# The seam between 50 recurrent steps and the score stores: counting on VectorE in the last step, both centrings first on ScalarE, and a later first split

## The chip, the cores and the metric

The kernel runs on one core of one Trainium2 chip. A core has TensorE (PE) for matrix products and transposes, VectorE (DVE), ScalarE (ACT) and GpSimd (POOL) for elementwise work, SyncE (SP), which here only issues transfers, and 16 DMA engines that carry them out. Matrix products land in PSUM; the other tiles on the core are in SBUF. The metric is the time of one execution on the device in microseconds (us).

## What is computed

A batch of 1024 sequences of 50 item numbers is turned into scores against 100001 items. Cut to what matters:

```python
emb = emb_table.at[0].set(0.0)                  # 100001 x 128
prefix = jnp.cumsum(emb[seq], axis=1)           # 1024 x 50 x 128
uF = prefix / jnp.minimum(t_idx, lengths)       # running mean of the items so far
y = (uF - mean) * rsqrt(var + 1e-5) * gamma + beta   # over the batch, for each step and feature
def step(v, x):                                 # 50 steps
    v = v + (x - v) / 2
    spike = (v - 1 >= 0)
    return v - spike, spike
scores = spikes.mean(axis=0) @ emb.T            # 1024 x 100001, 409.6 MB
```

Each step needs the one before it, since v is carried. The scores need the spike counts of all 50 steps.

## The kernel before

**Layout.** In the recurrent part the 128 features are the partitions and the 1024 sequences are the columns, so the mean and the variance over the batch are reductions along a row. v lives in PSUM (in turn in `v0` and `v1`), the counts in a bfloat16 tile `count`, and `negv` is the negative of v after its spikes are taken off. The order on each engine is as written in the program; nothing reorders it, and a semaphore wait is added wherever an instruction needs another engine's result, a buffer that is still read, or a PSUM bank that another engine is at.

**A step t.** Eight gathers of GpSimd (`gather`, L196) bring the rows of step t, two steps ahead, into one of two buffers `e`. PE transposes them onto the running sum `pre` (L309), which is two tiles of 512 columns, one for each half of the batch. VectorE makes `uF` from each half (L318) and its statistics (L319), then aggregates them to `mv` (L329). ScalarE takes a square root (L333) and centres `uF` (L340). VectorE makes the scale `a` by three tiny instructions, ScalarE applies it (`x`, L363), VectorE counts the spikes of the previous v (`spiked`, L289) and makes the new one (`step`, L366), and ScalarE makes `d`, v minus the threshold in bfloat16 (`over`, L282). `rest` (L286) on VectorE makes `negv` from d and v in the next step.

**The last step.** It is written apart, so that the first scores can start early. At its top GpSimd makes `s` from d (L303) and adds it to `count` (L304), which takes over the count of step 48's spikes. Between the two halves VectorE does `rest` and then `near` (L323), a piece of 128 columns that the first product needs. After `mv`, the first 128 sequences are finished by VectorE alone (`centred`, `vA`, `countA`); the other 896 go in two pieces, which ScalarE centres (L402) and scales (L363) one after the other, and which VectorE steps and counts into `countB` and `countC` (L366, L289). Sixteen transposes `warm` (L398) keep PE busy meanwhile.

**The scores.** The table is split into 98 parts of 1024 items. `prepare` transposes a part's rows on PE into PSUM (L124), ScalarE rounds them to a `hi` part (L146), and VectorE makes the remainder `lo` (L147); a product of 128 sequences by 512 items is two matmuls, with hi and with lo (`product`, L154). The first two parts are prepared inside steps 42 and 44. Blocks n of 128 sequences are worked through for groups of columns `WIDTHS`: the first groups have two parts, so a block is 128 x 2048. VectorE and ScalarE in turn scale 1024 columns from PSUM to an output tile `o` (L483, L485), and SyncE's queue issues its store (`store`, L163). Block 0 of the first group stands apart: four pieces of 512 columns, three scaled by ScalarE (L419) and the last by VectorE (L417), each stored at once. Block 1 stores 1024 columns at a time and later blocks the whole tile. There are four output tiles in the first groups, used in turn; a tile is refilled when its store has landed. `ready` prepares the next part when a hi and lo pair is free. In the first group one pair is free, so one part, the third, is prepared after block 2's store (L494), and the fourth when block 7 has set a pair free.

Of the kernel before, what the change touches and what calls it, by code (L numbers as in the profile page):

```python
# [12 lines left out]
F32 = mybir.dt.float32  # L13
# [5 lines left out]
ALU = mybir.AluOpType  # L19

P = 128
BN_EPS = 1e-5
V_TH = 1.0
HALF = 1024
KQ = HALF // P
BANK = 512
# [10 lines left out]
def rec_kernel(  # L37
# [124 lines left out]
    def store(n, c0, o):  # L162
        nc.sync.dma_start(out=outs[n, :, c0 : c0 + o.shape[1]], in_=o)  # L163


    with ExitStack() as ph:
# [118 lines left out]
        def rest(d, v):  # L285
            nc.vector.scalar_tensor_tensor(negv, d, 0.0, v, ALU.is_ge, ALU.subtract)  # L286
# [11 lines left out]
        for t in range(T):  # L298
            last = t == T - 1
            e = es.pop(t)  # L300
            if last:
                s = once.tile([P, B], F32, tag="zT", name="s")
                nc.gpsimd.tensor_single_scalar(s, d, 0.0, ALU.is_ge)  # L303
                nc.gpsimd.tensor_tensor(count, count, s, ALU.add)  # L304
            uF = up.tile([P, B], F32, tag="uF", name=f"uF_{t}")
            bs = sp.tile([P, B // BANK, 6], F32, tag="bs", name=f"bs_{t}")
            for h, cs in enumerate(halves):
                for k in range(0, BANK, P):
                    nc.tensor.matmul(  # L309
                        pre[h][:, k : k + P],  # L310
                        lhsT=e[:, h * BANK + k : h * BANK + k + P],
                        rhs=ident,
                        start=False,
                        stop=last,
                        is_transpose=True,
                        skip_group_check=True,
                    )
                nc.vector.scalar_tensor_tensor(uF[:, cs], rlen[:, cs], 1.0 / (t + 1), pre[h], ALU.max, ALU.mult)  # L318
                nc.vector.bn_stats(bs[:, h, :], uF[:, cs])  # L319
                if last and h == 0:  # L320
                    rest(d, v)
                    near = once.tile([P, P], F32, tag="r0", name="near")
                    nc.vector.tensor_scalar(near, negv[:, :P], -0.5, hgb[:, 1:2], ALU.mult, ALU.add)  # L323
            if t + 2 < T:
                gather(t + 2)
            if not last:
                correct(t + 1, l)
            mv = sp.tile([P, 2], F32, tag="mv", name=f"mv_{t}")
            nc.vector.bn_aggr(mv, bs.rearrange("p h s -> p (h s)"))  # L329


            r = sp.tile([P, 1], F32, tag="r", name=f"r_{t}")
            nc.scalar.activation(r, mv[:, 1:2], AF.Sqrt, bias=eps)  # L333
            if last:
                centred = once.tile([P, P], F32, tag="r0hi", name="centred")
                nc.vector.tensor_scalar(centred, uF[:, :P], mv[:, 0:1], hgb[:, 2:3], ALU.subtract, ALU.mult)
                w = sp.tile([P, 1], F32, tag="w", name="w")
                nc.vector.tensor_scalar_add(w, mv[:, 1:2], BN_EPS)
            else:
                nc.scalar.activation(uF, uF, AF.Identity, bias=mv[:, 0:1], scale=-1.0)  # L340


            if t and not last:
                rest(d, v)

            nc.vector.reciprocal(r, r)
            q = sp.tile([P, 1], F32, tag="q", name=f"q_{t}")
            a = sp.tile([P, 1], F32, tag="a", name=f"a_{t}")
            if last:
                nc.vector.tensor_scalar(q, w, r, r, ALU.mult, ALU.mult)  # L350
                nc.vector.scalar_tensor_tensor(q, q, 3.0, r, ALU.subtract, ALU.mult)
                vA = once.tile([P, P], F32, tag="r0n", name="vA")
                nc.vector.scalar_tensor_tensor(vA, centred, q, near, ALU.mult, ALU.add)
                spiked(countA, slice(0, P), vA)
                nc.vector.tensor_mul(a, q, hgb[:, 0:1])
            else:
                nc.vector.scalar_tensor_tensor(q, mv[:, 1:2], BN_EPS, r, ALU.add, ALU.mult)
                nc.vector.tensor_scalar(q, q, r, 3.0, ALU.mult, ALU.subtract)
                nc.vector.tensor_scalar(a, q, r, hgb[:, 0:1], ALU.mult, ALU.mult)


            def x(vt, cs):
                nc.scalar.activation(vt, uF[:, cs], AF.Identity, bias=hgb[:, 1:2], scale=a)  # L363

            def step(vt, cs):
                nc.vector.scalar_tensor_tensor(vt, negv[:, cs], -0.5, vt, ALU.mult, ALU.add)  # L366

            if not last:
                vt = vp.tile([P, B], F32, tag=f"v{t % 2}", name=f"v_{t}")
                x(vt, whole)  # L370
                if t:
                    spiked(count, whole, v)
                step(vt, whole)
                v = vt
                d = over(t, v)
                if t + 2 < T:
                    l = only(t + 2)

                if t in (T - 8, T - 6):
                    q = (t - T + 8) // 2  # L380
                    pair(q)
                    prepare(q, vp.tile([P, HALF], F32, tag="v1", name=f"pt_{q}"))
                    if q == TWICE - 1:
                        for k in range(TWICE):
                            rows[GROUP + k] = first[:, k, :]
                        nc.sync.dma_start(
                            out=first[:, :TWICE, :],
                            in_=table[GROUP * HALF : (GROUP + TWICE) * HALF, :].rearrange(
                                "(q p k) d -> p q (k d)", p=P, k=KQ
                            ),  # L390
                        )
# [8 lines left out]
        groups = [(slice(P, P + BANK), pre[1], countB), (slice(P + BANK, B), vC, countC)]  # L400
        for cs, vt, _ in groups:
            nc.scalar.activation(uF[:, cs], uF[:, cs], AF.Identity, bias=mv[:, 0:1], scale=-1.0)  # L402
            x(vt, cs)
        for cs, vt, c in groups:
            step(vt, cs)
            spiked(c, cs, vt)


        po0 = accp.tile([P, HALF], F32, tag="po0", name="po_0_0")
        po1 = vp.tile([P, HALF], F32, tag="v0", name="po_0_1")  # L410
        for q, (pool, tag, po) in enumerate(((gp, "e", po0), (up, "uF", po1))):
            o = pool.tile([P, HALF], F32, tag=tag, name=f"o_0_{q}")
            for h, cs in enumerate(halves):
                product(po[:, cs], q, 0, h * BANK, BANK)
            for h, cs in enumerate(halves):
                if q and h:
                    nc.vector.tensor_scalar_mul(o[:, cs], po[:, cs], 1.0 / T)  # L417
                else:
                    nc.scalar.mul(o[:, cs], po[:, cs], 1.0 / T)  # L419
                store(0, q * HALF + h * BANK, o[:, cs])  # L420

# [15 lines left out]
    for c, W in enumerate(WIDTHS):  # L439
# [30 lines left out]
        for n in range(NB):  # L470
            if c == 0 and n == 0:
                continue
            pool, tag, most = turns[blocks % len(turns)]
            blocks += 1
            o = pool.tile([P, most * HALF], F32, tag=tag, name=f"o_{c}_{n}")
            for q in range(q0, q1):
                h0 = (q - q0) * HALF
                hw = size(q)
                po = psum.tile([P, HALF], F32, tag="ps", name=f"po_{n}_{q}")
                for k0 in range(0, hw, BANK):  # L480
                    product(po[:, k0 : k0 + BANK], q, n, k0, min(BANK, hw - k0))
                if turn % 2 == 0:
                    nc.vector.tensor_scalar_mul(o[:, h0 : h0 + hw], po[:, :hw], 1.0 / T)  # L483
                else:
                    nc.scalar.mul(o[:, h0 : h0 + hw], po[:, :hw], 1.0 / T)  # L485
                turn += 1
                if c == 0 and n == 1:
                    store(n, q * HALF, o[:, h0 : h0 + hw])
                if n == NB - 1:
                    free.append(split.pop(q))  # L490
                    ready()
            if c or n > 1:
                store(n, q0 * HALF, o[:, : min(N, q1 * HALF) - q0 * HALF])
            if 2 <= n < NB - 1:  # L494
                ready()

            if n in (1, 4) and c >= MIDDLE and to_fetch < parts:
                g, k = divmod(to_fetch - TWICE, GROUP)
                if k or to_split >= (g - 1) * GROUP + TWICE:
                    if k == 0:  # L500
                        r = group(g)
                    fetch(r, to_fetch, GROUP // 2)
                    to_fetch += GROUP // 2
# [21 lines left out]
```

## Time and profile before

| | us |
|---|---|
| median of three timed runs (lowest, highest) | 1579.63 (1579.41, 1580.53) |
| the profiled execution | 1638.67 |
| its span, first to last instruction | 1636.5 |
| busy in the span: PE, VectorE, ScalarE, GpSimd | 1090.1, 942.9, 668.0, 388.3 |
| time of the chain that ended last spent on the score stores | 44% |
| mean rate of the transfers | 298 GB/s |

The profiled execution is 3.7% longer than the timed runs, so a time from the profile is used for differences and not for the whole. In the timelines below, times are microseconds from the start of the span; a row gives start, duration, engine, line, operation and operands, and in square brackets how long the engine had idled before and what released it. "remote" is a releaser that the profile couldn't name. The seam between the two stages is at about 577 us of this profile.

### The profile page before, as it was taken

What the parts mean: (1) busy time and instruction counts of PE and PEld (TensorE: products, weight loads), DVE (VectorE), ACT (ScalarE), POOL (GpSimd) and SP (SyncE); (2) the same over time, 40 slices, a digit from 0 to 9 for tenths busy, and PEclk for the clock granted to TensorE, in tenths of its full rate; (3) what the DMA queues carried; (4) which work ended last, traced back from release to release, by engine and by line L of the source; (5) the groups of instructions that cost most, each with busy time, mean ns of one, the idle gap of its engine ahead of it and who ended that gap; (6) DMA issues with size and microseconds to landing.
All of it is one profiled execution on the core that took longest, in us unless ns stands there. A gap on an engine that the chain in (4) does not pass through costs nothing.

```text
span 1636.5 us, 12239 instructions
## 1 busy us (share of the span) xinstructions
PE 1090.1 (67%) x4450; PEld 809.3 (49%) x4450; DVE 942.9 (58%) x1125; ACT 668.0 (41%) x697; POOL 388.3 (24%) x408
## 2 busy tenths in 40 slices
PE   4332334333343489898988788888778887888884
PEld 2111112111122267666866667666666666666663
DVE  5675667665575866565755555555545555555552
ACT  2332333333333355455544444444444444444442
POOL 7666676666766600000000000000000000000000
PEclk9999999999997599999999998999999999899998
DMA  9511111111112189999999999999999999999998
GB/s 347 213 47 45 45 50 48 45 45 47 52 45 59 51 358 416 402 421 414 409 423 435 427 429 423 419 429 425 413 429 412 429 421 420 426 411 417 412 427 344
DMA packets 51897, 488.12 MB, mean 298 GB/s; under 512 B 10075, under 2 KB 11004, under 8 KB 30588
## 3 DMA queue, kind: packets, MB, share of 16 engines
q1 hardware_dynamic: 30464, 429.81, 62.5%
q0 software_dynamic: 12800, 26.24, 6.0%
q10 hardware_dynamic: 8572, 31.28, 4.8%
q8 instruction: 35, 0.57, 0.1%
q14 instruction: 26, 0.21, 0.0%
HBM read 77.69 MB, written 409.60 MB: 298 GB/s over the span
## 4 chain that ended last, share of the span: by engine, by line
DMA 47%; PE 12%; DVE 11%; POOL 10%; another core or an unknown queue 7%; issue 6%; ACT 6%; ACTq 0%; SPq 0%; DVEq 0%; POOLq 0%
DMA scores<-o 44%; PE po L154 11%; POOL e L196 10%; ACT o L485 4%; DVE bs L319 2%; DVE uF L318 2%; DMA rows<-in_L_rec_emb_table 2%; DVE v L366 2%; DVE negv L286 1%; DMA e<-in_L_rec_emb_table,idx 1%; DVE o L483 1%; DVE count L289 1%; ACT v L363 1%; PE pt L124 1%
## 5 line engine op out<-in xcount | busy, mean ns | idle before, releaser
L483 DVE TENSOR_SCALAR o<-po 128x1024 f32<-128x1024 f32 x391 | 464.6, 1220 | 348.1 <-DMA scores<-o 313.8
L485 ACT ACTIVATE o<-po 128x1024 f32<-128x1024 f32 (+1 forms) x391 | 389.3, 1018 | 541.7 <-DMA scores<-o 326.3
L196 POOL DMA_INDIRECT e<-in_L_rec_emb_table,idx x400 | 382.7, 957 | 178.9 <-issue 115.9
L154 PE MATMUL po<-pairs,countB 128*128 128x512 f32 x1136 | 305.7, 415 | 64.2 <-ACT o L485 47.3
L154 PEld LDWEIGHTS po<-pairs,countB 128*128 128x128 f32 x1136 | 219.0, 198 | 126.9 <-ACT o L485 61.7
L154 PE MATMUL po<-pairs,countC 128*128 128x512 f32 x852 | 235.6, 423 | 47.3 <-ACT o L485 47.2
L270 PE MATMUL pre<-zT,ls 128*128 128x512 f32 x100 | 78.9, 791 | 257.1 <-DVE uF L318 211.3
L154 PEld LDWEIGHTS po<-pairs,countC 128*128 128x128 f32 x852 | 166.2, 201 | 92.8 <-ACT o L485 58.4
L309 PE MATMUL pre<-ident,e 128*128 128x128 f32 x400 | 129.3, 438 | 90.6 <-DMA e<-in_L_rec_emb_table,idx 70.7
L270 PEld LDWEIGHTS pre<-zT,ls 128*128 128x128 f32 x100 | 29.7, 298 | 294.8 <-DVE uF L318 238.2
L318 DVE SCALAR_TENSOR_TENSOR uF<-rlen,pre 128x512 f32<-128x512 f32 x100 | 68.0, 680 | 167.4 <-remote 126.8
L309 PEld LDWEIGHTS pre<-ident,e 128*128 128x128 f32 x400 | 79.9, 207 | 141.5 <-DMA e<-in_L_rec_emb_table,idx 107.7
L147 DVE TENSOR_TENSOR pairs<-pt,pairs 128x1024 fp32r<-128x1024 f32 x71 | 86.2, 1221 | 93.8 <-ACT pairs L146 93.7
L333 ACT ACTIVATE r<-mv,eps 128x1 f32<-128x1 f32 x50 | 14.8, 295 | 279.9 <-DVE mv L329 167.6
L124 PE MATMUL pt<-ident,rows 128*128 128x128 f32 x782 | 111.4, 289 | 8.4 <-issue 4.9
L124 PEld LDWEIGHTS pt<-ident,rows 128*128 128x128 f32 x782 | 101.0, 152 | 26.5 <-issue 12.5
L154 PE MATMUL po<-hi,countB 128*128 128x512 f32 x216 | 88.7, 411 | 18.6 <-ACT o L485 13.1
L154 PE MATMUL po<-lo,countB 128*128 128x512 f32 x216 | 85.6, 398 | 0.0
L282 ACT ACTIVATE d<-v,less 128x1024 bf16<-128x1024 f32 x49 | 54.5, 1113 | 63.5 <-DVE v L366 37.6
L154 PE MATMUL po<-hi,countC 128*128 128x512 f32 (+1 forms) x162 | 68.2, 421 | 17.1 <-ACT o L485 17.0
L146 ACT CAST pairs<-pt 128x1024 fp32r<-128x1024 f32 x71 | 71.8, 1011 | 15.2 <-PE pt L124 15.0
L154 PE MATMUL po<-pairs,countA 128*128 128x512 f32 x284 | 71.2, 394 | 7.4 <-ACT o L485 7.4
(78 smaller groups left out, 845.3 us busy)
## 6 DMA issues: line engine op xcount, KB each, us to landing
scores<-o SPq DMA_DIRECT2D x96, 3072.0 KB
scores<-o SPq DMA_DIRECT2D x32, 1536.0 KB
scores<-o SPq DMA_DIRECT2D x30, 1024.0 KB
rows<-in_L_rec_emb_table ACTq DMA_DIRECT2D x19, 1536.0 KB
scores<-o SPq DMA_DIRECT2D x8, 2896.5 KB
rows<-in_L_rec_emb_table SPq DMA_DIRECT2D x6, 3072.0 KB
e<-in_L_rec_emb_table,idx POOLq DMA_INDIRECT x400
rows<-in_L_rec_emb_table SPq DMA_DIRECT2D x1, 1024.0 KB
```

Of the source, the lines that this page charges most:

```text
L124: nc.tensor.transpose(pt[:, k0 : k0 + kw], r[:kw, k0 : k0 + D], ident[:kw, :kw])
L146: nc.scalar.copy(vh, vp)
L147: nc.vector.tensor_tensor(vl, vp, vh.bitcast(F32), ALU.subtract)
L154: nc.tensor.matmul(po[:, :kw], lhsT=counts[n], rhs=part[:, k0 : k0 + kw], start=j == 0, stop=j == 1,)
L196: nc.gpsimd.indirect_dma_start(out=es[t][:, n * P : (n + 1) * P], out_offset=None, in_=table, in_offset=bass.IndirectOffsetOnAxis(ap=idx[: ...
L270: nc.tensor.matmul(pre[h], lhsT=l, rhs=zT[:, h * BANK : (h + 1) * BANK], start=t == 0, stop=False, skip_group_check=True,)
L282: nc.scalar.activation(d, v, AF.Identity, bias=less)
L309: nc.tensor.matmul(pre[h][:, k : k + P], lhsT=e[:, h * BANK + k : h * BANK + k + P], rhs=ident, start=False, stop=last, is_transpose=True, ...
L318: nc.vector.scalar_tensor_tensor(uF[:, cs], rlen[:, cs], 1.0 / (t + 1), pre[h], ALU.max, ALU.mult)
L319: nc.vector.bn_stats(bs[:, h, :], uF[:, cs])
L483: nc.vector.tensor_scalar_mul(o[:, h0 : h0 + hw], po[:, :hw], 1.0 / T)
L485: nc.scalar.mul(o[:, h0 : h0 + hw], po[:, :hw], 1.0 / T)
```

## The change

In the last step, VectorE counts the spikes of step 48 (`spiked(count, whole, v)`), takes them off (`rest`) and makes `near`, all ahead of the two halves; GpSimd's two instructions are gone. After `mv`, ScalarE centres both pieces before it scales either. The products of block 0 are written ahead of the two calls of `x`, and ScalarE's scaling of the first 512 scores comes between the two calls of `x`, that of the second 512 after them, the rest after the counts. In the first group of columns, `ready` is called after blocks 4, 5 and 6, not after 2 to 6; since only one pair is free there, the third part is prepared two blocks later.

```diff
             if last:
-                s = once.tile([P, B], F32, tag="zT", name="s")
-                nc.gpsimd.tensor_single_scalar(s, d, 0.0, ALU.is_ge)
-                nc.gpsimd.tensor_tensor(count, count, s, ALU.add)
+                spiked(count, whole, v)
+                rest(d, v)
+                near = once.tile([P, P], F32, tag="r0", name="near")
+                nc.vector.tensor_scalar(near, negv[:, :P], -0.5, hgb[:, 1:2], ALU.mult, ALU.add)
...
                 nc.vector.bn_stats(bs[:, h, :], uF[:, cs])
-                if last and h == 0:
-                    rest(d, v)
-                    near = once.tile([P, P], F32, tag="r0", name="near")
-                    nc.vector.tensor_scalar(near, negv[:, :P], -0.5, hgb[:, 1:2], ALU.mult, ALU.add)
...
         for cs, vt, _ in groups:
             nc.scalar.activation(uF[:, cs], uF[:, cs], AF.Identity, bias=mv[:, 0:1], scale=-1.0)
+
+        po0 = accp.tile([P, HALF], F32, tag="po0", name="po_0_0")
+        po1 = vp.tile([P, HALF], F32, tag="v0", name="po_0_1")
+        o0 = gp.tile([P, HALF], F32, tag="e", name="o_0_0")
+        o1 = up.tile([P, HALF], F32, tag="uF", name="o_0_1")
+        firsts = [(q, po, o, h, cs) for q, po, o in ((0, po0, o0), (1, po1, o1)) for h, cs in enumerate(halves)]
+        for q, po, _, h, cs in firsts:
+            product(po[:, cs], q, 0, h * BANK, BANK)
+
+        def first_store(q, po, o, h, cs):
+            if q and h:
+                nc.vector.tensor_scalar_mul(o[:, cs], po[:, cs], 1.0 / T)
+            else:
+                nc.scalar.mul(o[:, cs], po[:, cs], 1.0 / T)
+            store(0, q * HALF + h * BANK, o[:, cs])
+
+        for k, (cs, vt, _) in enumerate(groups):
             x(vt, cs)
+            first_store(*firsts[k])
         for cs, vt, c in groups:
             step(vt, cs)
             spiked(c, cs, vt)
...
+        for f in firsts[2:]:
+            first_store(*f)
...
-            if 2 <= n < NB - 1:
+            if (2 if c else 4) <= n < NB - 1:
                 ready()
```

More of the change, by code (lines that the diff above doesn't have):

```diff
@@ L406, in rec_kernel @@
             spiked(c, cs, vt)
[L409 to L420, printed above, removed]
+        for f in firsts[2:]:
+            first_store(*f)
     psum = ctx.enter_context(
```

## The prediction

> **What bounds the kernel now.** I read the page first (slices, chain by line), then VectorE, ScalarE and GpSimd in order of time around the last step, then the windows in which the stores begin. The profiled execution took 1638.67 us (span 1636.5 and 2.2 around it). The median of the timed runs is 1579.63, 59 us less, so most times below are differences.
>
> From the page, engine rows over 40 equal slices, and the chain by line:
>
> ```profile
> span 1636.5 us, 12239 instructions
> ...
> POOL 7666676666766600000000000000000000000000
> ...
> DMA  9511111111112189999999999999999999999998
> ...
> L196 POOL DMA_INDIRECT e<-in_L_rec_emb_table,idx x400 | 382.7, 957 | 178.9 <-issue 115.9
> ```
>
> There are two stages. Until about 577 us GpSimd issues 400 gathers for the 50 recurrent steps (0.957 us busy and 0.30 us of issue each: 8 per step, 10.04 us), and the transfer engines are nearly empty. After that they are full until the end, moving the score stores. The changed work lies on the seam. A microsecond saved before the stores begin, or a hole closed in their first microseconds, is worth a microsecond at the end; nothing else in the diff can be.
>
> VectorE in order of time (start, duration, line, out<-in, idle time before it), then ScalarE and GpSimd:
>
> ```profile
> 562.56 1.23 DVE L366 SCALAR_TENSOR_TENSOR v<-negv,v 128x1024 f32<-128x1024 f32 x1 [0.20 <-issue]
> 566.84 0.69 DVE L318 SCALAR_TENSOR_TENSOR uF<-rlen,pre 128x512 f32<-128x512 f32 x1 [3.05 <-remote]
> 567.56 0.69 DVE L319 BATCH_NORM_STATS2 bs<-uF 128x6 f32<-128x512 f32 x1
> 568.17 1.20 DVE L286 SCALAR_TENSOR_TENSOR negv<-d,v 128x1024 f32<-128x1024 bf16 x1
> 569.41 0.70 DVE L323 TENSOR_SCALAR near<-negv,hgb 128x128 f32<-128x128 f32 x1
> 570.03 0.68 DVE L318 SCALAR_TENSOR_TENSOR uF<-rlen,pre 128x512 f32<-128x512 f32 x1
> 571.47 0.21 DVE L329 BATCH_NORM_AGGREGATE mv<-bs 128x2 f32<-128x12 f32 x1
> 571.71 0.35 DVE L336 TENSOR_SCALAR centred<-uF,mv,hgb 128x128 f32<-128x128 f32 x1
> ```
> ```profile
> 563.83 1.11 ACT L282 ACTIVATE d<-v,less 128x1024 bf16<-128x1024 f32 x1 [1.30 <-DVE v L366]
> 565.03 2.78 POOL L303 TENSOR_SCALAR s<-d 128x1024 f32<-128x1024 bf16 x1 [2.11 <-ACT d L282]
> 567.89 2.14 POOL L304 TENSOR_TENSOR count<-count,s 128x1024 bf16<-128x1024 bf16 x1
> ```
>
> Call V = 563.79 the end of the last v, and M = 571.68 the end of mv, so M = V+7.89. The line at 566.84 matters most: VectorE idled 3.05 us before the first half, then did negv and near (1.94 us from 568.17 to 570.11) between the halves, on the path.
>
> The start of the stores, one row per window (columns: window, length, busy time of PE, PE weight loads, VectorE, ScalarE, GpSimd, clock, transfer share, GB/s):
>
> ```profile
> 576.00:578.00 2.00, 1.19 (x5) 0.67 (x5) 1.71 (x4) 1.20 (x3) 0.00 (x0) 1.00 0.44 167
> 578.00:580.00 2.00, 2.00 (x9) 1.66 (x10) 1.05 (x1) 0.66 (x1) 0.00 (x0) 1.00 0.99 378
> ...
> 582.00:584.00 2.00, 2.00 (x10) 1.64 (x9) 1.00 (x1) 1.21 (x3) 0.00 (x0) 1.00 0.88 367
> 584.00:586.00 2.00, 2.00 (x10) 1.62 (x9) 2.00 (x3) 1.17 (x2) 0.00 (x0) 1.00 0.69 270
> 586.00:588.00 2.00, 2.00 (x11) 1.64 (x10) 1.71 (x2) 1.14 (x2) 0.00 (x0) 1.00 0.93 373
> ```
>
> Transfers fill at about 577.2, dip between 582 and 588 (0.24 + 0.62 + 0.14 = 1.0 us lost), and are full from then on.
>
> **What the Trainium skill says.** (1) "PSUM — Partial Sum Buffer", section "PSUM bank collisions raise a hardware error": two engines must not touch one bank and quadrant at once, two reads included. v lies in PSUM, so VectorE's count of it can't run beside ScalarE's d, which reads v. The trace agrees as far as it goes: nothing on VectorE reads v between 563.83 and 564.94. The changed program has this wait: the count waits on ScalarE, and negv behind it no longer does. (2) "SBUF — State Buffer", section "Who interferes with whom": a VectorE tensor_scalar from SBUF to SBUF can take the port pair that GpSimd uses, exclusively, and the loser blocks for the whole instruction. The trace agrees: near took 0.70 us beside GpSimd's count and ended with it (570.11 against 570.03); centred, the same operation and shape, took 0.35 with GpSimd idle.
>
> **The change part by part.**
>
> Part 1, counting and negv ahead of the halves. GpSimd's two instructions (2.78 and 2.14 us) go. They were no step of the profiled path: countA, which waits for them, began at 573.20, they ended at 570.03. VectorE gets one count of 128x1024 (1.22 us, the row of the regular step), and its order becomes count, negv, near, half, half. d ends at V+1.15, so count V+1.2 to 2.4, negv to 3.6 (1.17), near to 4.0 (0.35), first half uF from V+4.05. By the spacing of the profile (0.72, 0.69, 0.72, 0.73, 0.21 with gaps) mv ends at V+7.1. Queued behind the new wait on VectorE are negv, near and both halves; PE's 16 warm-up transposes wait for negv, now over at V+3.6 against V+5.6, so they finish sooner. Against the profile: 7.89 - 7.1 = 0.8 us gained.
>
> In the timed runs I don't expect the 3.05 us stall. Its releaser is unknown, and PE's last transposes of that half ended near 560.0; such stalls are about as much as GpSimd's idle time beyond issue, 178.9 - 115.9 = 63 us, close to the 59 us that the timed runs lack. Without it V follows the previous second half by 6.13 us (557.66 to 563.79), and the next second half is ready 10.04 us after that one, at V+3.9. Then before: first half V to V+1.4, negv to 2.6, near held by GpSimd's s until about V+4.0 and done at 4.4, second half from there, M = V+6.1. centred then meets GpSimd's count (to V+6.5) and may lose up to 0.5. So before stands at V+6.1 to 6.6, after at V+7.1: 0.5 to 1.0 us lost. If near instead loses the port to both GpSimd instructions (V+6.2, done at 6.6), before is V+8.2 and the change gains 1.1. I take a loss of 0.4, ends -1.1 (gain) and +1.5 (near not held at all: M = V+5.6).
>
> Part 2, ScalarE. Before, the second piece's centring (0.60) ran after the first x; now it fits into ScalarE's 1.05 us wait for a. The first store's scaling moves ahead of the second x. It starts at M+2.7 instead of M+3.96 and the first store goes out about 1.25 us sooner. That alone fills nothing: each early store is 256 KB, 0.65 us of transfer, and the next must keep up. VectorE's chain (step, countB, step, countC, then the fourth piece and the first 1024 columns of block 1) is the same and was nearly gapless from 574.49; it only loses its 0.26 us wait on ScalarE. The fifth store moves from M+7.4 to M+7.2, and PE's next product, which waited for that fourth piece (577.98), with it. Worth 0.2 us.
>
> Part 3, the split. Only the first column group changes, and in it only one split: the third part's pair is the only free one. Its 8 transposes (1.04 us PE), hi (1.01 ScalarE) and lo (1.22 VectorE) move from before block 3 to after block 4. Block 3's VectorE half stood behind lo (583.00 to 584.22) and its store went out at 585.42; that is the dip. Now PE reaches that block 1.0 us sooner and its store goes out at about M+12.0 = 583.7 of the old clock; the engines are then still busy with block 2 until M+13.65, where before block 3's data began at M+14.65. Parts 2 and 3 together: 1.0 us. The moved split is covered by the stores queued: block 5's store at M+17.25 (0.9 us from issue to data, as at 576.25 to 577.17) meets a queue that lasts to M+18.85. If that cover, 0.7 us, were gone, a hole up to 1.2 us (lo) would come back.
>
> **Sum.** Against the profiled execution: 0.8 + 1.0 = 1.8 us, 1638.7 to 1636.9. For the median: +0.4 - 1.0 = -0.6, so 1579.0 us.
>
> **The rivals.** A measurement can tell about 0.2% of this kernel, 3.16 us, from no change.
> A, the likeliest: the gather spacing hides half of the moved VectorE work, the dip goes: 1579.0.
> B, the stall is real in timed runs: negv and near come off the path, 0.8 to 2.0 us by how late the half is, plus 1.0: 1577.8 down to 1576.6. For it: the 3.05 us idle; against it: the 59 us. With the near-blocked case (1.1 + 1.0) it gives 1577.5.
> C, slower: the count's wait for d. If both halves are ready early and near was never held, before stood at V+5.6 and after at V+7.1; 1.5 - 1.0 gives 1580.1, and without the closed dip 1581.1. It decides as soon as the second half is ready before V+5.4, the time at which VectorE is free for it.
> D, nothing from parts 2 and 3, since the transfers take the holes back at the later dips (a share of 0.91 between 760 and 780): 1580.0.
> E, a gain of 3.2 us or more: B in full with the early stores also counting 0.5 or more.
>
> **Chances.** A 0.36, B 0.20, C 0.12, D 0.11, E 0.12; the last 0.09 is a new hole in the transfers that I don't see, slower than 1582.8. A to D lie within 0.2%; I add 0.05 to faster for B's far end and 0.04 to slower for C's, since the timed stall and the port are both unseen. So faster 0.17, same 0.70, slower 0.13. The range, 1575.8 to 1581.8, holds A to D and the near part of E and of the new hole; some 0.09 lies beyond each end.
>
> **What would show it.** The count on VectorE at L289 starting when d ends (about V+1.2, not V), near at 0.35, both uF halves 1.4 us apart, mv at V+7.1. ScalarE's second centring directly behind the first, ahead of a. Windows 10 to 18 us after M at a share near 1.0, and lo behind block 4. Wrong if mv comes before V+6.5, if the count doesn't wait for d, or if a dip appears about 17 us after M.

## The result and the profile after

The changed kernel takes 1575.91 us (median of 12 runs, 1575.22 to 1576.95) where the kernel before took 1579.61 on the same chip (12 runs, 1579.18 to 1580.53): ratio 0.9977, interval 0.9968 to 0.9986. It is 3.7 us faster. The prediction was 1579.0, so the sign was right and the size was a sixth of what came.

The profile shown before, of 1638.67 us, was an execution with 13 long gaps between gathers, 54 us in all beyond their usual spacing. Experiment e1 gave one of the same kernel without them (1580.10 us, span 1578.0), and after is compared with that one. The page after, slices and groups:

```profile
span 1573.8 us, 12233 instructions
...
POOL 7777777777776000000000000000000000000000
...
L196 POOL DMA_INDIRECT e<-in_L_rec_emb_table,idx x400 | 379.8, 949 | 123.8 <-issue 112.8
```

The same group in e1's profile of the kernel before:

```profile
L196 POOL DMA_INDIRECT e<-in_L_rec_emb_table,idx x400 | 382.4, 956 | 123.8 <-issue 116.4
```

The number behind the busy time is the mean of one gather: 949 ns against 956. GpSimd idled 123.8 us before its gathers in both, so the 2.6 us of busy time are the whole difference. The 400 gathers are what sets the end of the first stage, and none of them is touched by the diff.

VectorE in order of time after (start, duration, line, operands, idle before):

```profile
501.80 1.23 DVE L363 SCALAR_TENSOR_TENSOR v<-negv,v 128x1024 f32<-128x1024 f32 x1 [0.20 <-ACT v L360]
504.21 1.22 DVE L289 SCALAR_TENSOR_TENSOR count<-v,count 128x1024 bf16<-128x1024 f32 x1 [1.18 <-ACT d L282]
505.35 1.21 DVE L286 SCALAR_TENSOR_TENSOR negv<-d,v 128x1024 f32<-128x1024 bf16 x1
506.59 0.29 DVE L305 TENSOR_SCALAR near<-negv,hgb 128x128 f32<-128x128 f32 x1
...
509.56 0.21 DVE L326 BATCH_NORM_AGGREGATE mv<-bs 128x2 f32<-128x12 f32 x1
509.80 0.34 DVE L333 TENSOR_SCALAR centred<-uF,mv,hgb 128x128 f32<-128x128 f32 x1
...
511.43 0.15 DVE L352 TENSOR_TENSOR a<-q,hgb 128x1 f32<-128x1 f32 x1
```

V, the end of the last v, is 503.03, and the count waits 1.18 us for ScalarE's d. M, the end of mv, is at V+6.74, and `a`, used below as a time, is the end of its row, V+8.55. VectorE and GpSimd in e1's profile of the kernel before:

```profile
504.37 1.23 DVE L366 SCALAR_TENSOR_TENSOR v<-negv,v 128x1024 f32<-128x1024 f32 x1 [0.21 <-ACT v L363]
...
506.83 1.20 DVE L286 SCALAR_TENSOR_TENSOR negv<-d,v 128x1024 f32<-128x1024 bf16 x1
508.07 0.55 DVE L323 TENSOR_SCALAR near<-negv,hgb 128x128 f32<-128x128 f32 x1
509.59 0.69 DVE L318 SCALAR_TENSOR_TENSOR uF<-rlen,pre 128x512 f32<-128x512 f32 x1 [0.97 <-PE pre L309]
...
511.04 0.21 DVE L329 BATCH_NORM_AGGREGATE mv<-bs 128x2 f32<-128x12 f32 x1
511.29 1.29 DVE L336 TENSOR_SCALAR centred<-uF,mv,hgb 128x128 f32<-128x128 f32 x1
...
513.92 0.15 DVE L355 TENSOR_TENSOR a<-q,hgb 128x1 f32<-128x1 f32 x1
```
```profile
507.47 2.80 POOL L303 TENSOR_SCALAR s<-d 128x1024 f32<-128x1024 bf16 x1
510.36 2.15 POOL L304 TENSOR_TENSOR count<-count,s 128x1024 bf16<-128x1024 bf16 x1
```

Here V is 505.60. The first half was not late (the 3.05 us stall of the first profile is gone), VectorE idled 0.97 us for PE's last transpose of the second half, M came at V+5.65, and then `centred` took 1.29 us, until GpSimd's count ended at 512.51. So `a` came at V+8.48, as late as after.

ScalarE after, behind M:

```profile
510.00 1.21 ACT L399 ACTIVATE uF<-uF,mv 128x512 f32<-128x512 f32 x2
511.70 0.78 ACT L360 ACTIVATE pre<-uF,hgb,a 128x512 f32<-128x512 f32 x1 [0.49 <-DVE a L352]
512.86 0.60 ACT L413 ACTIVATE o<-po 128x512 f32<-128x512 f32 x1 [0.38 <-PE po L154]
513.35 0.67 ACT L360 ACTIVATE vC<-uF,hgb,a 128x384 f32<-128x384 f32 x1
```

Both centrings fit ahead of `a`, and the first score piece is scaled before the second piece of the batch. Windows after (the last three columns are PE's clock, the transfer share and GB/s), 12 to 18 us after M, and the window 14 us after M of e1's kernel before:

```profile
521.76:523.76 2.00, 2.00 (x15) 1.75 (x14) 1.09 (x1) 1.22 (x2) 0.00 (x0) 1.00 1.06 426
523.76:525.76 2.00, 2.00 (x11) 1.61 (x9) 1.26 (x2) 1.18 (x2) 0.00 (x0) 1.00 0.94 385
525.76:527.76 2.00, 2.00 (x10) 1.63 (x9) 2.00 (x2) 1.20 (x2) 0.00 (x0) 1.00 1.03 426
```
```profile
525.25:527.25 2.00, 2.00 (x11) 1.61 (x10) 2.00 (x3) 1.18 (x2) 0.00 (x0) 1.00 0.65 262
```

The dip is closed. From these two executions, by the end of the last transfer (1580.14 and 1576.04):

| stretch | before (e1) | after | difference |
|---|---|---|---|
| start to V | 505.60 | 503.03 | -2.57 |
| V to `a` | 8.48 | 8.55 | +0.07 |
| `a` to the end of the transfers | 1066.06 | 1064.46 | -1.60 |

The sum is -4.1; the medians say -3.7. Most of it lies ahead of all the work that the change touches. Some 0.65 us of the 1.60 are not the change's: PE's clock at the seam was half in e1 and full from V+8 in after, and it differs between executions of one kernel (after and e11, below, are one kernel; in e11 it was half until V+12).

### The profile page after: what moved, and what is told of

Its sections match the earlier page's. It is cut to its first block, busy times and chain, and to the rows that moved or that the text cites. A ratio compares the mean times of both kernels' runs of the same rounds, so it can differ in the third digit from the quotient of the medians.

```text
span 1573.8 us, 12233 instructions
## 1 busy us (share of the span) xinstructions
PE 1128.7 (72%) x4450; PEld 801.0 (51%) x4450; DVE 944.8 (60%) x1126; ACT 668.2 (42%) x697; POOL 380.4 (24%) x406
## 4 chain that ended last, share of the span: by engine, by line
DMA 51%; POOL 18%; PE 11%; issue 8%; ACT 5%; DVE 3%; another core or an unknown queue 1%; ACTq 0%; SPq 0%; POOLq 0%; DVEq 0%
DMA scores<-o 46%; POOL e L196 18%; PE po L154 11%; DMA e<-in_L_rec_emb_table,idx 5%; ACT o L488 5%; DVE o L486 1%; PE pt L124 0%; ACT pairs L146 0%; DMA idx<-in_r_seq 0%; PE pre L310 0%; ACTq L116 0%; DVE negv L286 0%; DVE bs L320 0%; ACT hi L146 0%
## 5 line engine op out<-in xcount | busy, mean ns | idle before, releaser
L196 POOL DMA_INDIRECT e<-in_L_rec_emb_table,idx x400 | 379.8, 949 | 123.8 <-issue 112.8
L310 PE MATMUL pre<-ident,e 128*128 128x128 f32 x400 | 179.8, 462 | 228.9 <-DMA e<-in_L_rec_emb_table,idx 228.3
L310 PEld LDWEIGHTS pre<-ident,e 128*128 128x128 f32 x400 | 73.3, 184 | 338.8 <-DMA e<-in_L_rec_emb_table,idx 338.1
L360 ACT ACTIVATE v<-uF,hgb,a 128x1024 f32<-128x1024 f32 x49 | 59.2, 1208 | 30.6 <-DVE a L356 30.5
```

The source lines that it names most:

```text
L196: nc.gpsimd.indirect_dma_start(out=es[t][:, n * P : (n + 1) * P], out_offset=None, in_=table, in_offset=bass.IndirectOffsetOnAxis(ap=idx[: ...
L310: nc.tensor.matmul(pre[h][:, k : k + P], lhsT=e[:, h * BANK + k : h * BANK + k + P], rhs=ident, start=False, stop=last, is_transpose=True, ...
```

## The experiments

V, M, the times from V and the median gather come from one profiled execution of each (medians of 944 and 952 go with the means of 949 and 956 above); "first data" is when the first score transfer began. The change is given against the median of the kernel before, in runs on the same chip (1579.93 for e1 to e4, 1580.89 for e5 to e8, 1642.43 for e9 to e11, 1642.37 for e12).

| | median us | change | ratio (interval) | gather ns | V | M | `a` | first data |
|---|---|---|---|---|---|---|---|---|
| after | 1575.91 | -3.70 | 0.9977 (0.9968-0.9986) | 944 | 503.03 | V+6.74 | V+8.55 | V+11.32 |
| e1 | 1579.88 | -0.05 | 1.0001 (0.9992-1.0009) | 952 | 505.60 | V+5.65 | V+8.48 | V+12.12 |
| e2 | 1577.78 | -2.15 | 0.9982 (0.9974-0.9989) | 944 | 503.20 | V+6.74 | V+8.55 | V+12.11 |
| e3 | 1579.65 | -0.28 | 0.9999 (0.9991-1.0008) | 952 | 506.06 | V+5.44 | V+8.33 | V+11.10 |
| e4 | 1579.09 | -0.84 | 0.9994 (0.9985-1.0002) | 952 | 505.96 | V+5.55 | V+8.40 | V+11.96 |
| e5 | 1576.46 | -4.43 | 0.9974 (0.9963-0.9984) | 944 | 503.18 | V+5.63 | V+7.44 | V+10.99 |
| e6 | 1577.15 | -3.74 | 0.9976 (0.9967-0.9986) | 947 | 503.88 | V+6.74 | V+8.55 | V+12.19 |
| e7 | 1577.14 | -3.75 | 0.9978 (0.9970-0.9986) | 944 | 503.19 | V+6.73 | V+8.54 | V+11.30 |
| e8 | 1575.51 | -5.38 | 0.9969 (0.9958-0.9980) | 947 | 504.12 | V+5.54 | V+7.35 | V+10.61 |
| e9 | 1639.91 | -2.52 | 0.9987 (0.9977-0.9996) | 952 | 567.29 | V+5.61 | V+7.81 | V+10.57 |
| e10 | 1640.44 | -1.99 | 0.9990 (0.9974-1.0006) | 955 | 575.07 | V+6.74 | V+8.55 | V+11.29 |
| e11 | 1641.47 | -0.96 | 0.9987 (0.9976-0.9999) | 947 | 576.69 | V+6.74 | V+8.55 | V+12.19 |
| e12 | 1641.67 | -0.70 | 0.9995 (0.9981-1.0009) | 944 | 568.36 | V+6.74 | V+8.55 | V+11.30 |

### The change taken apart

**e1**, the kernel before, unchanged.

> The kernel before, unchanged, for a profile of an execution without the long stalls. Port theory (near waits for GpSimd): near on VectorE at L323 takes well over 0.35 us or starts late, and mv ends 8.0 to 8.4 us after the last v, against 6.74 in the changed kernel. Theory of the transfers (the gain lies in the first stores): mv ends 5.6 to 6.6 us after the last v, so the last step is no slower than in the changed kernel, and the stores show more than 2 us of holes. Time: as before, within 0.5 us of 1579.6.

It shows the last step without a stall, as quoted above: `near` took 0.55 us while s ran from 507.47 to 510.27. It was not held until s had ended.

**e2**, the first part alone: the last step's new order on VectorE, without GpSimd.

```diff
-                s = once.tile([P, B], F32, tag="zT", name="s")
-                nc.gpsimd.tensor_single_scalar(s, d, 0.0, ALU.is_ge)
-                nc.gpsimd.tensor_tensor(count, count, s, ALU.add)
+                spiked(count, whole, v)
+                rest(d, v)
...
```

> Only the last step changed: count, negv and near on VectorE ahead of the halves, GpSimd does nothing there; ScalarE's order and the split as before. Port theory: 1.4 to 2.6 us faster than before. Theory of the transfers: 0 to 1 us slower than before.

The size, -2.15 us, is in the range of the port theory, and the theory is wrong all the same. M came at V+6.74, 1.1 us later than before, and `a` where it had been. What moved is V: 503.20 against 505.60.

**e3**, ScalarE's order alone.

```diff
         for cs, vt, _ in groups:
             nc.scalar.activation(uF[:, cs], uF[:, cs], AF.Identity, bias=mv[:, 0:1], scale=-1.0)
...
+        for k, (cs, vt, _) in enumerate(groups):
             x(vt, cs)
+            first_store(*firsts[k])
```

> Only ScalarE's order after mv changed: both centrings first, the first store's scaling between the two x. Port theory: 0.2 us faster. Theory of the transfers: 0.5 to 1.5 us faster, since four stores start earlier.

**e4**, the split alone.

```diff
-            if 2 <= n < NB - 1:
+            if (2 if c else 4) <= n < NB - 1:
```

> Only the third part's split moved from block 2 to block 4. Port theory: 0.8 to 1.0 us faster (the dip between 582 and 588 us of the first profile). Theory of the transfers: 1.5 to 3 us faster.

e3 and e4 are compared with each other and with e2, since PE's clock was full at the seam in all three (1.00 from V+4 on) and half in e1 (0.50 to 0.54 from V+4 to V+12). With the new order the first data came 0.86 us sooner (V+11.10 against V+11.96). With the moved split the share 14 to 16 us after M was 1.02, without it 0.66. What counts is how much of the time from `a` to V+40 the transfers did not fill, summed from the records of the transfers: 4.63 us in e2, which has neither part, 4.54 in e3, 3.79 in e4, 3.71 in after. So the order is worth 0.1 us there, the split 0.8, both 0.9. The clock weighs as much: e1 lacked 5.28, and e6 and e11, which have after's seam but had half the clock until V+12, lacked 4.57 and 4.68. Neither part is resolved in the timed runs alone (both intervals hold 1). With the first part they make -3.70 against -2.15, but those two were not timed on one chip and their intervals overlap.

### What GpSimd's two instructions cost

**e5**, the kernel before without the two instructions.

```diff
-            if last:
-                s = once.tile([P, B], F32, tag="zT", name="s")
-                nc.gpsimd.tensor_single_scalar(s, d, 0.0, ALU.is_ge)
-                nc.gpsimd.tensor_tensor(count, count, s, ALU.add)
```

> The kernel before without GpSimd's two instructions of the last step and with nothing in their place, so that the spikes of the step before the last are left out of the count. Gather theory (the mere presence of GpSimd's two instructions in the program makes each of the 400 gathers about 7 ns longer, 0.956 against 0.949 us on average): gathers at 0.949, the end of the last v 2.5 us earlier (503.1), and the last step itself quicker too, since nothing holds centred: M at V+5.5, a about 1.0 us nearer to V than in the kernel before (V+7.4); 3.5 us gained, 1576.4. Theory of the last step (GpSimd's work delays near and centred, the gathers are the same): gathers at 0.956, V at 505.6, 1.0 us gained, 1578.9.

Both effects show here. M is the same as in e1 (V+5.63 and V+5.65), `centred` took 0.34 us and not 1.29, and `a` came 1.04 us sooner; V came 2.4 us sooner. The predicted 3.5 us became 4.4. PE's clock was full from V+8, and from `a` to V+40 the transfers lacked 0.64 us less than in e1; the rest isn't traced, and the kernel before has no profile from e5's chip. The row of `centred` in e5:

```profile
508.85 0.34 DVE L332 TENSOR_SCALAR centred<-uF,mv,hgb 128x128 f32<-128x128 f32 x1
```

**e6** and **e7**, the kernel after with one tiny GpSimd instruction behind the last gather.

```diff
+            if last:
+                z = sp.tile([P, 1], F32, tag="z", name="z")
+                nc.gpsimd.tensor_single_scalar(z, eps, 0.0, ALU.is_ge)
```

> The kernel after plus one GpSimd instruction of the same operation as s, on a tile of 128x1, behind the last gather; nothing reads it. Gather theory: gathers back at 0.956, V back at 505.6, about 2.5 us slower than the kernel after (1578.4), though the instruction itself takes about 0.1 us and nothing waits for it. Theory of the last step: as the kernel after, 1575.9, gathers at 0.949.

e7 has `nc.gpsimd.tensor_tensor(z, eps, eps, ALU.add)` in that place.

> The same with an instruction of the other operation, an addition of two 128x1 tiles, in place of the comparison. Gather theory: 1578.4 and 0.956 again if any computing instruction does it; if only one of e6 and this one does, it is the operation; if neither does, it takes both or it takes their size or their waits. Theory of the last step: 1575.9.

Both kept the short gathers (947 and 944 ns) and the gain of the kernel after (3.74 and 3.75 us against 3.70), though the instruction took 0.25 us in e6 and 0.20 in e7, more than the 0.1 expected. The gather theory in its first form, that any computing instruction lengthens them, fell.

**e9**, the kernel after with GpSimd's two instructions back in place of VectorE's count.

```diff
-                spiked(count, whole, v)
+                s = once.tile([P, B], F32, tag="zT", name="s")
+                nc.gpsimd.tensor_single_scalar(s, d, 0.0, ALU.is_ge)
+                nc.gpsimd.tensor_tensor(count, count, s, ALU.add)
                 rest(d, v)
```

> The kernel after with GpSimd's two instructions of the kernel before (s, then count) in place of VectorE's count; negv and near stay ahead of the halves on VectorE. The 400 gathers ahead of them are the same instructions as in every other kernel. Theory of the two whole instructions (something about their size, their waits or their number lengthens the gathers that stand ahead of them in GpSimd's program): gathers at 0.956 us, V at about 505.6, and centred held by the second one; about 1578.5. Theory of chance (gathers differ from one execution or one build to the next, whatever stands behind them): gathers near 0.950, V at 503.0 to 504.1, and the time set by the last step alone, 1576.0 to 1577.5.

The gathers were long again, 952 ns. Since VectorE has no count here, `a` came at V+7.81, sooner than after.

**e10**, the kernel after with the same two operations, and their waits, on tiles of one column.

```diff
...
+                nc.gpsimd.tensor_single_scalar(z, d[:, :1], 0.0, ALU.is_ge)
+                nc.gpsimd.tensor_tensor(z, z, z, ALU.add)
```

> The kernel after plus two GpSimd instructions behind the last gather, with the operations and the waits of s and count (the first waits for ScalarE's d, the second for the first) but on tiles of 128x1; nothing reads them. If the number of GpSimd's instructions or their waits lengthen the gathers: 0.956 us, V at 505.6, 2.5 us slower than the kernel after. If it is their size, or chance: 0.949 to 0.952, time as the kernel after.

**e11**, the kernel after, unchanged, on the same chip.

> The kernel after unchanged, on the chip of the two others. Theory of the two whole instructions: gathers 0.949 to 0.952 again. Theory of chance: any value from 0.949 to 0.957 may come. Either way the ratio to the kernel before should be 0.9977 within its interval, if the change is worth the same on this chip.

**e12**, the kernel after with four tiny comparisons.

```diff
...
+                for k in range(4):
+                    z = sp.tile([P, 1], F32, tag=f"z{k}", name=f"z_{k}")
+                    nc.gpsimd.tensor_single_scalar(z, eps, 0.0, ALU.is_ge)
```

> The kernel after plus four GpSimd comparisons on 128x1 tiles of their own behind the last gather, which wait for none of each other and not for ScalarE; nothing reads them. GpSimd's program then has as many instructions as in the kernel before. If the number of instructions behind the gathers lengthens them: median gather 0.952 to 0.955 us. If it takes the two operations together or their waits: 0.944 to 0.947 us, as with none or one. The time tells little if this chip has stalls of 60 us in the gathers; without them 1578.4 or 1576 to 1577.

These chips stall in the gathers as the first profile did (the kernel before takes 1642 us there, and its runs spread over 10 us), so times say little: in e9 to e12 I read the gathers. In the times of that chip the longer gathers don't show: e9 and e10 took 1639.91 and 1640.44 us, e11 1641.47, with intervals of 0.1 to 0.16% to each side. Minimum, median and maximum of one gather in ns, from the view of the tile `e`, for e10, e11 (same chip) and e12:

```profile
L196 POOL DMA_INDIRECT e<-in_L_rec_emb_table,idx x400: 949/955/1687, 3.5 to 563.5; - x134
```
```profile
L196 POOL DMA_INDIRECT e<-in_L_rec_emb_table,idx x400: 942/947/2315, 3.2 to 564.2; - x134
```
```profile
L196 POOL DMA_INDIRECT e<-in_L_rec_emb_table,idx x400: 938/944/2319, 3.4 to 564.1; - x134
```

With two instructions of 0.2 us, which run after all the gathers and for which nothing waits, the median gather was 8 ns longer on one chip (955 against 947). Spans on GpSimd are rough in these profiles, but the spacing from one gather's start to the next says the same: its median was 1.260 us in e10 and 1.252 in e11, 1.257 in e1 and 1.249 in after. Over all the profiles the medians fall apart without overlap: 952 to 955 ns in the six with both a comparison and an addition of GpSimd behind the gathers, 944 to 947 in the eight with neither, one of them, or four comparisons. One kernel gave 944 on one chip (after) and 947 on another (e11), so differences of 3 ns come without a change of the kernel; the two groups lie 5 or more apart. So it is neither size (e10) nor the number of instructions (e12). Whether it takes the two different operations, one GpSimd instruction that waits for another, or one that waits for ScalarE's d (all six have all three, none of the eight has any) isn't told apart, and why it reaches back to earlier gathers is open.

8 ns times 399 is 3.2 us; after has one early gather of 2.32 us where e1's longest is 1.70, which leaves 2.6, and V moved 2.57 between e1 and after, 2.40 between e1 and e2 on one chip.

### A better place for the count

**e8**, the kernel after with VectorE's order changed.

```diff
-            if last:
-                spiked(count, whole, v)
-                rest(d, v)
...
                 nc.vector.bn_stats(bs[:, h, :], uF[:, cs])
+                if last and h == 0:
+                    rest(d, v)
+                    near = once.tile([P, P], F32, tag="r0", name="near")
+                    nc.vector.tensor_scalar(near, negv[:, :P], -0.5, hgb[:, 1:2], ALU.mult, ALU.add)
+                    spiked(count, whole, v)
```

> The kernel after with VectorE's order changed: first half, negv, near, count, second half, so that the 1.2 us of the count stand where VectorE of the kernel before waited 0.97 us for the second half, and the first half no longer stands behind ScalarE's d. GpSimd computes nothing, as in the kernel after. First half from V, negv from V+1.45, near, count to V+4.2, second half to V+5.6, mv by V+5.85 instead of V+6.74. If the gathers (0.949) and the last step add up: 0.9 us quicker than the kernel after, 1575.0. If the kernel after's gain were in its order of count and negv ahead of the halves: slower than the kernel after, 1576.5 or more.

VectorE of e8, in order of time:

```profile
506.59 0.29 DVE L319 TENSOR_SCALAR near<-negv,hgb 128x128 f32<-128x128 f32 x1
506.79 1.22 DVE L289 SCALAR_TENSOR_TENSOR count<-v,count 128x1024 bf16<-128x1024 f32 x1
508.00 0.69 DVE L314 SCALAR_TENSOR_TENSOR uF<-rlen,pre 128x512 f32<-128x512 f32 x1
```

The count fills the wait for the second half (0.97 us in e1, 1.21 in e5), and nothing waits for d. M is at V+5.54 and `a` 1.2 us sooner than after. The time is 5.4 us below the kernel before, 1575.51. e6 and e7, which are after with one tiny instruction more, took 1577.15 and 1577.14 on the same chip. But the intervals of the ratios overlap (0.9958 to 0.9980 against 0.9968 to 0.9986 for after, which wasn't timed on that chip), so e8's lead over after is shown by the trace, not yet by the timed runs.

## Why the prediction was right or wrong

**The 59 us.** Right. The timed runs of before and after had no such stalls, and on two chips of the experiments they were there again. The 3.05 us stall ahead of the first half is absent from e1, so rival B's premise fell.

**Part 1, the loss of 0.4: right in its net effect to 0.3 us by luck, since its errors cancel, and it left out the main term.** M after came at V+6.74 where I had V+7.1, because consecutive VectorE instructions overlap a little more than the spacings I added. M before came at V+5.65 where I had V+6.1 to 6.6: I had `near` held by GpSimd's s until V+4.0 or later, and it ended at V+3.0. So at M the change lost 1.09 us, and rival C's premise was true: the second half was ready at V+4.0 and `near` wasn't held for long. But `centred`, which I let lose "up to 0.5", was held for 0.95 us to the end of GpSimd's count. That returned the whole loss: +0.07 at `a`.

On the Trainium skill's "SBUF — State Buffer", section "Who interferes with whom": that the loser blocks for the whole instruction holds for the addition L304 in every trace that shows it (`near` 0.70 in the first profile, `centred` 1.29 in e1 and 0.67 in e9, each ending within 0.1 us of L304's end), and not for the whole of the comparison L303, which lasts 2.8 us: beside it `near` took 0.29 in e9, as it does alone, and 0.55, 0.41 and 0.47 in e1, e3 and e4. In these three it ended 1.14 to 1.16 us after L303's start, so it looks held for a first part; why isn't shown. The measurement decides; I had used the rule for both. The wait for d, from "PSUM — Partial Sum Buffer", section "PSUM bank collisions raise a hardware error", came as forecast: V+1.18 for V+1.2.

**The step that failed** is "GpSimd's two instructions (2.78 and 2.14 us) go. They were no step of the profiled path". True of their busy time, and of the place where they stand; but with them went 8 ns of each of the 400 gathers ahead, -2.57 us at V. No case of mine held that the first stage could change. This alone is two thirds of the gain, and it is what carries the result just past the 0.2% at which I put the bound of "same". That 1575.91 still lies in the range of 1575.8 to 1581.8 is luck: that end of it stood for rivals B and E, whose reasons did not occur.

**Part 2, worth 0.2.** The mechanism came as written: centrings back to back, first scaling ahead of the second x. The first data came 0.86 us sooner (e3 against e4) where I had the first store 1.25 sooner. Most of that was lost again in a deeper dip, as "that alone fills nothing" has it: 0.1 us was left by V+40. In timed runs alone -0.28, inside the noise.

**Part 3, the dip.** Right as far as the dip goes: `lo` ran at 524.50, behind block 4, the share in the dip went from 0.65 to 0.94, and no hole appeared about 17 us after M (1.03). Parts 2 and 3 together I had at 1.0; where PE's clock was alike they filled 0.92 us by V+40 (4.63 less 3.71). The medians give 1.55 (3.70 less 2.15, on two chips), the stretch from `a` to the end 1.60, in which the clock has a share of some 0.65 (5.28 in e1 less 4.63 in e2).

**Rival D** (holes taken back later) is not ruled out in part. From V+40 on the transfers lacked 11.50 us in e1 and 11.49 in after, but over all profiles 10.9 to 11.5 in the five with the old split and 11.2 to 12.3 in the nine with the moved one, 0.6 more in the mean, so part of the closed dip may come back later. The timed gain of the split alone, 0.84, has an interval that holds both no gain and all of it. **Rival E** had the size, not its reasons: it needed B in full. **The sum**: predicted +0.4 - 1.0 = -0.6; by the trace -2.57 + 0.07 - 1.60 = -4.1; without the clock's 0.65 it is -3.4, and the medians say -3.7.

## What to carry to other kernels

Before you price a removed instruction by its busy time, find the repeated instruction that bounds the same engine, and after the result compare its mean duration first: 8 ns times 400 outweighed everything that this diff rearranged. A work item that has to go somewhere belongs in a measured wait of the engine that takes it, here the one for the second half, and not ahead of it: that put `a` 1.2 us sooner. A part whose timed gain matches a theory hasn't shown the theory; e2 matched, and only the times of V, M and `a` told why.

## What the runs showed of the hardware

- GpSimd's gathers of 128 rows took 952 to 955 ns (median) in programs where a comparison and an addition of GpSimd, which waited for ScalarE, came later in its queue, even on tiles of one column (955 in e10), and 944 to 947 in the others. The cause is open.
- On two of the chips that ran the experiments the gathers stalled: 13 or 14 gaps of 3.0 to 6.8 us from one gather's start to the next, often 32 gathers apart, where 1.25 is usual: 54 to 58 us more in all (e9 to e12). In the profiles from the two other chips (e1 to e8) no gap was above 2.7 us. The kernel before takes 1642 us on the first two, 1580 or 1581 on the others.
- A VectorE instruction of 128x128 waited for the end of GpSimd's addition in bfloat16 (1.29 us in e1, 0.34 in e5 without it), while beside GpSimd's comparison one took 0.29 to 0.55 us (e9, e1).
- PE's clock at the seam was half in some executions and full in others; where it was still half from V+8 to V+12 (e6, e11) the first data came at V+12.19 and where it was full (after, e7, e10, e12) at V+11.30, with the same M.
